# Weights and keys of the later stages prepared in steps inside the stage ahead

## The chip, the cores and the metric

The kernel runs on one core of a Trainium2 chip. The metric is the device time of one execution in microseconds (us), as the median of several runs. The engines are named PE (TensorE, the matrix unit; PEld is its weight load), DVE (VectorE), ACT (ScalarE), POOL (GpSimd) and SP (SyncE, which here only issues DMAs).

## The reference

The network has four layers, each an attention over a context of 1601 rows and a feed-forward part, all with 256 columns and residual sums over 2048 tokens. The parts that the change touches are these:

```python
def _L1_xattn_ref(h1, h2, mask, Wq, Wk, Wv):
    Q = jnp.einsum('bnd,hd->bnh', h1, Wq)
    K = jnp.einsum('bmd,hd->bmh', h2, Wk)
    V = jnp.einsum('bmd,od->bmo', h2, Wv)
    E = jnp.einsum('bnh,bmh->bnm', Q, K)
    E = jnp.where(mask == 0, jnp.float32(-10000000000.0), E)
    A = jax.nn.softmax(E / math.sqrt(HID), axis=2)
    return jnp.einsum('bnm,bmo->bno', A, V)

def _bitlinear(x, w_latent):                      # ffn of layer 1
    scale = jnp.clip(jnp.mean(jnp.abs(w_latent), axis=1, keepdims=True), 1e-05, None)
    tern = jnp.clip(jnp.round(w_latent / scale), -1.0, 1.0)
    return x @ (tern * scale).T
h = _bitlinear(x, w_fc) + gate * (x @ v.T @ fast_b.T @ u.T)
y = _bitlinear(jnp.maximum(h, 0.0) ** 2, w_proj)

def _ternary_linear(x, w):                        # ffn of layer 2
    alpha = jnp.mean(jnp.abs(w))
    w_t = jnp.sign(w) * (jnp.abs(w) > 0.5 * alpha)
    rms = jnp.sqrt(jnp.sum(x * x, axis=-1, keepdims=True)) / jnp.sqrt(d)
    return jnp.einsum('bsd,fd->bsf', x / (rms + EPS), w_t)
y = _ternary_linear(gelu(_ternary_linear(x, w_up)), w_down)
```

Layer 2's attention has the same form without a mask and with biases. Layer 3's attention has 16 heads of 16 columns, a mask, biases and an output projection; its masked keys get minus infinity. In both layers with a mask, every row of the drawn masks is zero for at least the first 1201 keys, so that only the last 400 of the 1601 context rows can count.

## The kernel before

The tokens lie in SBUF for the whole run, as 16 tiles of 128 rows (`x0` to `x15`), and the transposed context too (`ctxT`). Each stage goes over four chunks of 512 tokens. `norm` normalizes a chunk (statistics and scaling on DVE, the power on POOL), transposes it on PE into a PSUM buffer `pm` and lets ACT copy it out; with `split` it makes a high part on ACT and the rest on DVE. Each stage opens PSUM pools with `banks`: usually two buffers each of `psc` (scores or hidden units, two banks each), `pm` (small things) and `pa` (accumulators).

The stages follow each other in `network`. The first attention also looks at both masks, and a branch on the result (`tc.If`) picks the fast side: a tail attention over the last 400 keys (`attention1_tail`, L812 to L920), `ffn1` (L957), the attention over all keys (`attention1`, L654), `ffn2` (L1122), the last attention over the tail (`attention3_tail`, L1429), and `ffn3`. The other side is for other masks and doesn't run here.

In an attention, weights are transposed (`transpose_weight`, L211), keys and values made for all context rows, and then chunk by chunk: queries `q` with a bf16 copy `qb`, row maxima with bf16 matmuls (L881 or L748, reduced on DVE), scores (L903 or L780), the exponential on ACT, and value matmuls into `pa` (L913 or L800), whose result DVE divides and adds to `x`. The next chunk's queries and maxima come from a generator (`prepare`) that `step` advances a little between the current chunk's scores and value matmuls.

`ffn1` first loads its weights, then makes ternary weights on DVE (`ternary`: one comparison into `lo`, L928, and a comparison and subtraction, L929), transposes them on PE in bf16 (`transpose_up`, L938, and `transpose_down`, L950) with ACT copies out of PSUM, and prepares a low-rank term (`u`, `fast_b`, `b4`, `vh`, `vl`). Only then does the loop over chunks start, with low-rank matmuls (L1052), up matmuls (L1078) and down matmuls (L1115). `ffn2` does the same with thresholds over a whole matrix (L1141 to L1145), no low-rank term, a Gelu on ACT, and, per chunk, a sum of squares `sq` that POOL adds up (L1186) and PE sums over columns (L1197). `attention3_tail` transposes four weights (L211, L1503), makes keys with biases (L1511 to L1517) and values (L1521), and then walks over 16 units of a chunk and four heads each, projecting queries at L1545.

The order on each engine is made by a scheduler while the kernel is built, from the dependencies and the order in the source. Where a stage is opened with `manual_schedule(engines={PE})`, as the chunk loops of `ffn1` and `ffn2` are, PE keeps the source's order; in the last attention's loop all engines do. At run time each engine takes its instructions in the built order. Raw weights come through SP's DMA queue into `wraw`, a pool of three buffers used in turn (`weights`, L195), so a load waits until the weights three requests earlier have been used up. A pool opened inside a stage lies where the stage ahead had its own tiles, and its first uses wait until those are free:

```python
with ExitStack() as s:                                   # ffn1, L965
    self.banks(s)
    pool = s.enter_context(tc.tile_pool(name="f1", bufs=1))
...
net.attention1_tail("L1_xattn", masks[0])                # network, L1747
net.ffn1()
net.attention1("L2_xattn", bias=True)
net.ffn2()
net.attention3_tail(masks[1])
```

Of the kernel before, what the change touches and what calls it, by code (L numbers as in the profile page):

```python
# [15 lines left out]
P = 128  # L16
# [38 lines left out]
class Net:  # L55
# [44 lines left out]
    def psc(self):  # L100
        return self.ps_s.tile([P, 2, 512], F32, tag="s", name="psc")

# [102 lines left out]
    def transpose_weight(self, dst, raw, pad=None):  # L205

        nc = self.nc
        for kc in range(2):
# [5 lines left out]
            if pad:  # L214
                nc.scalar.copy(
                    dst[:, kc, :].rearrange("p (h e) -> p h e", e=32)[:, :, 0:16],
                    ps[:, :D].rearrange("p (h e) -> p h e", e=16),
                )
            else:
                nc.scalar.copy(dst[:, kc, :], ps[:, :D])  # L220

# [432 lines left out]
    def attention1(self, pre, mask=None, bias=False):  # L654
# [5 lines left out]
        with ExitStack() as s:  # L660
# [108 lines left out]
            for c in range(NCH):  # L769
# [25 lines left out]
                for i in range(TPC):  # L795
                    x = self.x[c * TPC + i]
                    acc = self.pa()
                    for kt in range(NKT):
# [5 lines left out]
                        if kt % 6 == 5:  # L804
                            step(nxt, 1)
                    ri = self.small.tile([P, 1], F32, name="ri1")
# [5 lines left out]
    def attention1_tail(self, pre, mask):  # L812
# [5 lines left out]
        with ExitStack() as s:  # L818
# [75 lines left out]
            for c in range(NCH):  # L894
# [14 lines left out]
                for i in range(TPC):  # L909
# [7 lines left out]
                    step(nxt, 1)  # L917
                    ri = self.small.tile([P, 1], F32, name="ri1")
# [12 lines left out]
    def transpose_up(self, dst, t):  # L931

        nc = self.nc
        for kc in range(2):
            for j in range(2):
# [5 lines left out]
                nc.scalar.copy(dst[:, kc, j * 512 : (j + 1) * 512], ps)  # L941

    def transpose_down(self, dst, t):

        nc = self.nc
        for f in range(0, 8, 2):
# [7 lines left out]
            nc.scalar.copy(dst[:, f : f + 2, :], ps.rearrange("p (k o) -> p k o", k=2))  # L954


    def ffn1(self):  # L957
# [6 lines left out]
        self.load_rows("L1_ffn_w_proj", F, wpr)  # L964
        with ExitStack() as s:  # L965
            self.banks(s)
            pool = s.enter_context(tc.tile_pool(name="f1", bufs=1))
            tp = s.enter_context(tc.tile_pool(name="f1t", bufs=3))
            hp = s.enter_context(tc.tile_pool(name="f1h", bufs=2))
            u = pool.tile([P, NF, R], F32, name="u")  # L970
            vv = pool.tile([R, D], F32, name="vv")
            fb = pool.tile([R, R], F32, name="fb")
            gate = pool.tile([R, 1], F32, name="gate")
            nc.sync.dma_start(u, a["L1_ffn_u"].rearrange("(o p) r -> p o r", p=P))
            nc.sync.dma_start(vv, a["L1_ffn_v"])
            nc.sync.dma_start(fb, a["L1_ffn_fast_b"])
            nc.sync.dma_start(gate, a["L1_ffn_gate"].partition_broadcast(R))

            def scales(view, n, cols):
                sc = pool.tile([P, n], F32, name=f"sc{n}")  # L980
                half = pool.tile([P, n], F32, name=f"half{n}")
                nhalf = pool.tile([P, n], F32, name=f"nhalf{n}")
                nc.vector.tensor_reduce(sc, view, AX.X, ALU.add, apply_absolute_value=True)
                nc.vector.tensor_scalar(sc, sc, 1.0 / cols, 1e-5, ALU.mult, ALU.max)
                nc.vector.tensor_scalar(half, sc, 0.5, None, ALU.mult)
                nc.vector.tensor_scalar(nhalf, sc, -0.5, None, ALU.mult)
                return sc, half, nhalf


            sc1, half, nhalf = scales(wfc, NF, D)  # L990
            rs1 = pool.tile([P, NF], F32, name="rs1")
            nc.vector.reciprocal(rs1, sc1)
            tfc = pool.tile([P, NF, D], BF16, name="tfc")
            for o in range(NF):
                self.ternary(tp, tfc[:, o, :], wfc[:, o, :], half[:, o : o + 1], nhalf[:, o : o + 1])
                nc.vector.tensor_scalar(u[:, o, :], u[:, o, :], rs1[:, o : o + 1], None, ALU.mult)
            wfT = pool.tile([P, 2, F], F32R, name="wfT")
            self.transpose_up(wfT, tfc)


            uT = pool.tile([R, F], F32, name="uT")
            b = pool.tile([R, F], F32, name="b")
            bh = pool.tile([R, 2, F], F32R, name="bh")
            b4 = pool.tile([P, F], F32R, name="b4")
            nc.gpsimd.memset(b4.bitcast(F32), 0.0)
            for j in range(2):
                ps = self.pm()
                for i in range(4):
                    nc.tensor.transpose(ps[0:R, i * P : (i + 1) * P], u[:, 4 * j + i, :], self.ident)
                nc.scalar.copy(uT[:, j * 512 : (j + 1) * 512], ps[0:R, :])  # L1010
                ps = self.pm()
                nc.tensor.matmul(ps[0:R, :], lhsT=fb, rhs=uT[:, j * 512 : (j + 1) * 512], start=True, stop=True)
                nc.vector.tensor_scalar(b[:, j * 512 : (j + 1) * 512], ps[0:R, :], gate, None, ALU.mult)
            nc.vector.tensor_copy(bh[:, 0, :], b)
            nc.vector.tensor_tensor(bh[:, 1, :], b, bh[:, 0, :].bitcast(F32), ALU.subtract)
            for k in range(4):
                nc.scalar.copy(b4[32 * k : 32 * k + R, :], bh[:, k % 2, :])

            v4 = pool.tile([P, 2, P], F32, name="v4")
            nc.gpsimd.memset(v4, 0.0)  # L1020
            vh = pool.tile([P, 2, P], F32R, name="vh")
# [100 lines left out]
    def ffn2(self):  # L1122
# [8 lines left out]
        with ExitStack() as s:  # L1131
# [23 lines left out]
            for o in range(2):  # L1155
                self.ternary(tp, tdn[:, o, :], wdn[:, o, :], half, nhalf)
# [638 lines left out]
```

## Time and profile before

| what | value |
| --- | --- |
| median of 3 runs | 2196.48 us (2189.63 to 2197.22) |
| the profiled execution | 2192.32 us, its span 2190.6 us |
| busy in the span | PE 1934.6 us (88%), DVE 1203.5 (55%), ACT 715.5 (33%), POOL 628.6 (29%) |
| chain that ended last | PE 65%, DVE 20%, ACT 5%, DMA 4% |
| mean granted PE clock | 0.946 |

The page shows one execution. Busy time is the time in which an engine executes; the rows of a stretch give it for each engine, with the number of instructions, and then PEclk, the granted clock of TensorE as a share of full speed. A line of the timeline has the start in us, the length in us, the engine, the source line and operation, what is written and read, and in brackets the idle time before it and what ended it. An f32 matmul shows as two records[...].

### The profile page before, as it was taken

Reading aid. Unit: us, or ns where it says so; the run is one execution under the profiler, and the core shown is the slowest. Engines: PE = TensorE matmul, PEld = TensorE weight load, DVE = VectorE, ACT = ScalarE, POOL = GpSimd, SP = SyncE. Lnnn points to the kernel's source line nnn. Section 1 sums busy time; section 2 is a strip of 40 time slices with the busy share of each in tenths; the row PEclk is TensorE's granted clock in tenths of the full one; section 3 lists DMA queues with packets and bytes.
Section 4 is the critical chain, followed back from the end, with each engine's and each line's share of the span. In section 5 each row is a group of like instructions: output and inputs, shape, how many; then the busy total and the mean of one; then the engine's idle time right before and its main releaser. Section 6 shows DMA issues by size and latency. Waiting matters only on the chain.

```text
span 2190.6 us, 22795 instructions
## 1 busy us (share of the span) xinstructions
PE 1934.6 (88%) x8831; PEld 963.6 (44%) x8841; DVE 1203.5 (55%) x2252; ACT 715.5 (33%) x968; POOL 628.6 (29%) x405
## 2 busy tenths in 40 slices
PE   7789999999998587789898789999977879889899
PEld 3233333333333433234444575455566622333487
DVE  4565656556462599985645553322156558677400
ACT  4554434444443100000011442111133246555422
POOL 1168878778686000000001011000013301111210
PEclk9799999999999599999998799999988889999999
DMA  8820000000000000000200000000000000000361
GB/s 280 274 82 1 1 1 1 1 1 1 1 1 0 0 1 1 1 0 0 68 0 14 27 1 22 1 0 1 0 1 1 5 1 1 1 1 1 107 199 62
DMA packets 39699, 63.51 MB, mean 29 GB/s; under 512 B 5134, under 2 KB 32159, under 8 KB 39583
## 3 DMA queue, kind: packets, MB, share of 16 engines
q1 hardware_dynamic: 37776, 60.33, 8.5%
q10 hardware_dynamic: 1806, 1.64, 0.2%
q8 instruction: 71, 1.16, 0.2%
q14 instruction: 46, 0.37, 0.1%
HBM read 59.87 MB, written 2.10 MB: 28 GB/s over the span
## 4 chain that ended last, share of the span: by engine, by line
PE 65%; DVE 20%; ACT 5%; DMA 4%; issue 4%; POOL 2%; SPq 0%; ACTq 0%; DVEq 0%; POOLq 0%
PE pa L468 7%; PE psc L456 5%; PE psc L641 5%; PE psc L780 4%; PE pa L800 4%; DVE ge L590 4%; PE psc L1578 3%; DVE mp L381 3%; DVE ge L592 3%; PE psc L1716 3%; PE pa L1727 3%; DVE ri L418 2%; ACT p L1585 2%; PE psc L454 2%; PE pm L1545 1%
## 5 line engine op out<-in xcount | busy, mean ns | idle before, releaser
L477 POOL TENSOR_TENSOR sp<-sp,p 128x1024 f32<-128x1024 f32 (+1 forms) x176 | 418.2, 2376 | 60.1 <-ACT p L461 49.5
L381 DVE TENSOR_REDUCE mp<-pm 128x1 f32<-128x512 f32 x384 | 242.6, 679 | 160.6 <-PE pm L376 159.8
L461 ACT ACTIVATE p<-psc 128x1024 f32<-128x1024 f32 (+1 forms) x208 | 212.7, 1022 | 259.5 <-PE psc L456 161.9
L456 PE MATMUL psc<-qT,kT 64*128 64x512 f32 (+1 forms) x832 | 221.7, 594 | 0.0
L468 PE MATMUL pa<-p,v 128*64 128x512 f32 (+1 forms) x832 | 202.4, 608 | 0.0
L607 PE MATMUL psc<-ge,pick 128*8 128x512 bf16 x512 | 142.3, 378 | 37.7 <-DVE ge L590 18.6
L1585 ACT ACTIVATE p<-psc 100x1024 f32<-100x1024 f32 x128 | 124.0, 1021 | 75.8 <-PE psc L1578 73.1
L1564 DVE TENSOR_REDUCE ms<-psc 128x2 bf16<-128x800 f32 x128 | 122.7, 981 | 43.3 <-PE psc L1560 41.4
L376 PE MATMUL pm<-kb,qb 64*128 64x512 bf16 x384 | 101.0, 391 | 27.2 <-DVE mp L381 25.7
L144 POOL TENSOR_SCALAR rstd<-mv 128x4 f32<-128x4 f32 x32 | 8.7, 272 | 358.1 <-DVE mv L140 358.1
L641 PE MATMUL psc<-w_e,xe 128*128 128x512 f32 x256 | 110.4, 593 | 0.0
L468 PEld LDWEIGHTS pa<-p,v 128*64 128x64 f32 (+1 forms) x832 | 50.9, 137 | 129.4 <-issue 126.4
L843 POOL MEMSET v<- 128x4 f32 x1 | 0.1, 104 | 364.3 <-DVE n_odd L294 364.3
L780 PE MATMUL psc<-q,kT 128*128 128x512 f32 (+1 forms) x208 | 102.2, 610 | 0.0
L590 DVE TENSOR_SCALAR ge<-bc,g 128x128 bf16<-128x128 f32 (+15 forms) x128 | 99.8, 780 | 1.8 <-ACT bc L584 1.8
L456 PEld LDWEIGHTS psc<-qT,kT 64*128 64x128 f32 (+1 forms) x832 | 86.0, 185 | 19.5 <-issue 6.3
L800 PE MATMUL pa<-v,p 128*128 128x257 f32 (+1 forms) x416 | 93.9, 381 | 0.2
L607 PEld LDWEIGHTS <-pick 128*8 128x8 bf16 x512 | 39.4, 85 | 117.1 <-issue 91.1
L454 PE MATMUL psc<-sh,negz 64*128 64x512 bf16 (+1 forms) x416 | 87.7, 384 | 3.6 <-ACT sh L403 3.5
L592 DVE TENSOR_SCALAR ge<-bc,g 128x1920 bf16<-128x1920 f32 (+14 forms) x120 | 89.4, 747 | 1.0 <-ACT bc L584 1.0
L753 DVE TENSOR_REDUCE mp<-pm 128x1 f32<-128x512 f32 x64 | 34.3, 570 | 99.9 <-PE pm L748 90.6
L648 DVE SCALAR_TENSOR_TENSOR x<-psc,g,x 128x256 f32<-128x256 f32 x128 | 61.9, 484 | 46.1 <-PE psc L641 42.5
(343 smaller groups left out, 3260.4 us busy)
## 6 DMA issues: line engine op xcount, KB each, us to landing
w<-in_L_ffn_w_dram SPq DMA_DIRECT2D x16, 1024.0 KB, 6.9
head<-in_mask_BxSxS_ik_dram SPq DMA_DIRECT2D x16, 600.5 KB, 4.0
head<-in_mask_1x1xSxS_ik_dram SPq DMA_DIRECT2D x16, 600.5 KB, 4.9
tail<-in_mask_BxSxS_ik_dram SPq DMA_DIRECT2D x16, 200.0 KB, 4.2
tail<-in_mask_1x1xSxS_ik_dram SPq DMA_DIRECT2D x16, 200.0 KB, 3.8
x<-in_x_dram SPq DMA_DIRECT2D x16, 128.0 KB, 3.7
w_e<-in_L_ffn_experts_dram SPq DMA_DIRECT2D x2, 1024.0 KB, 7.4
out_dram<-y SPq DMA_DIRECT2D x16, 128.0 KB, 2.5
```

The costliest lines, as they stand in the source:

```text
L381: nc.vector.tensor_reduce(mp[:, i, j, n : n + 1], pair[j][:, :wd], AX.X, ALU.max)
L456: nc.tensor.matmul(sc[:r, j, :], lhsT=kT[h, hp, kt * P : kt * P + r], rhs=q[h, :], start=False, stop=True,)
L461: nc.scalar.activation(p[:r], sc[:r], AF.Exp, scale=DH**-0.5)
L468: nc.tensor.matmul(acc[h, :], lhsT=v[:r, kt, hp * P + h.start : hp * P + h.stop], rhs=p[:r, j, :], start=kt == 0, stop=kt == NKT - 1,)
L477: nc.gpsimd.tensor_tensor(sums[:r], sums[:r], p[:r], ALU.add)
L590: nc.vector.tensor_scalar(ge[:, :hi], bc[:, :hi], own, None, ALU.is_lt)
L592: nc.vector.tensor_scalar(ge[:, hi:], bc[:, hi:], own, None, ALU.is_le)
L607: nc.tensor.matmul(rk[j // 2][0:E, j % 2, :], lhsT=pick[:, e, :], rhs=ge[:, j * CH : (j + 1) * CH], start=first, stop=last,)
L641: nc.tensor.matmul(sc[:, j, :], lhsT=xnT[t // TPC][:, kc, (t % TPC) * P : (t % TPC + 1) * P], rhs=ew[kc][:, half * 4 + 2 * j : half * 4 + ...
L780: nc.tensor.matmul(sc[:r, j, :], lhsT=kT[:, kc, ks], rhs=q[:, kc, :], start=kc == 0, stop=False)
L800: nc.tensor.matmul(acc[:, : D + 1], lhsT=p[:r, kt, i * P : (i + 1) * P], rhs=v[:r, kt, :], start=kt == 0, stop=kt == NKT - 1,)
L1585: nc.scalar.activation(p[:TR], sc[k][:TR], AF.Exp, scale=DH**-0.5)
```

## The change

The preparation of `ffn1`, of `ffn2` and of the last attention becomes a generator each: `ffn1_weights`, `ffn2_weights` and `attention3_keys`. Each loads its raw weights and opens its pools at its first step, in an `ExitStack` that `network` holds open around two stages; the later steps do the same work as before in small portions. The stage ahead gets the generator as `beside` and advances it: the tail attention by two steps after the value matmuls of each row block, the long attention by one, and `ffn2` by two for each pair of hidden blocks. `finish` runs what is left. The chunk loops themselves are the same. The raw weights are now requested before those of the attention in front of them. The last attention's values weight gets its own tile. The side of the branch that doesn't run here does its preparation at once, as before.

```diff
+    def finish(self, steps):
+        with ExitStack() as s:
+            self.banks(s)
+            drain(steps)
...
     def transpose_weight(self, dst, raw, pad=None):
+        drain(self.transpose_weight_steps(dst, raw, pad))
+    def transpose_weight_steps(self, dst, raw, pad=None):
...
+            yield
...
-    def attention1(self, pre, mask=None, bias=False):
+    def attention1(self, pre, mask=None, bias=False, beside=None):
...
+                    step(beside, 1)
                     ri = self.small.tile([P, 1], F32, name="ri1")
...
-    def attention1_tail(self, pre, mask):
+    def attention1_tail(self, pre, mask, beside=None):
...
                     step(nxt, 1)
+                    step(beside, 2)
...
-    def ffn1(self):
+    def ffn1_weights(self, s):
...
         self.load_rows("L1_ffn_w_fc", D, wfc)
         self.load_rows("L1_ffn_w_proj", F, wpr)
+        pool = s.enter_context(tc.tile_pool(name="f1", bufs=1))
+        tp = s.enter_context(tc.tile_pool(name="f1l", bufs=2))
...
+        yield
...
+        sc1, half, nhalf = scales(wfc, NF, D)
...
+        for o in range(NF):
+            self.ternary(tp, tfc[:, o, :], wfc[:, o, :], half[:, o : o + 1], nhalf[:, o : o + 1])
+            nc.vector.tensor_scalar(u[:, o, :], u[:, o, :], rs1[:, o : o + 1], None, ALU.mult)
+            if o % 2:
+                yield
+        wfT = pool.tile([P, 2, F], F32R, name="wfT")
+        yield from self.transpose_up(wfT, tfc)
...
+        for o in range(2):
+            self.ternary(tp, tpr[:, o, :], wpr[:, o, :], half[:, o : o + 1], nhalf[:, o : o + 1])
+            yield
+        wpT = pool.tile([P, NF, D], F32R, name="wpT")
+        yield from self.transpose_down(wpT, tpr)
...
+        self.f1 = wfT, wpT, b4, vh, vl, sc1, scb
+    def ffn1(self):
+        wfT, wpT, b4, vh, vl, sc1, scb = self.f1
...
+    def ffn2_weights(self, s):
...
+        for o in range(0, NF, 4):
+            yield
+            self.ternary(tp, tflat[:, o * D : (o + 4) * D], wflat[:, o * D : (o + 4) * D], half, nhalf)
...
+    def ffn2(self, beside=None):
...
                     if f == 2 and c + 1 < NCH:
                         nxt = self.norm(c + 1, rms=True, split=hp)
+                    step(beside, 2)
...
+    def attention3_keys(self, mask, s):
...
+        for w, n, pad in ((wkT, "Wk", True), (wqT, "Wq", True), (wvT, "Wv", None)):
+            yield from self.transpose_weight_steps(w, raw[n], pad)
...
+            nc.tensor.matmul(ps[:, :NTAIL], lhsT=to17, rhs=away, start=False, stop=True)
+            nc.scalar.activation(kT[:, g, :], ps[:, :NTAIL], AF.Identity, bias=kbias[:, g : g + 1])
+            nc.vector.tensor_copy(kb[:, g, :], kT[:, g, :])
+            yield
...
+        self.k3 = spread, qbias, bo, wqT, woT, kT, kb, v, ms
...
-        net.attention1_tail("L1_xattn", masks[0])
-        net.ffn1()
-        net.attention1("L2_xattn", bias=True)
-        net.ffn2()
-        net.attention3_tail(masks[1])
+        with ExitStack() as s1:
+            later = net.ffn1_weights(s1)
+            step(later, 1)
+            net.attention1_tail("L1_xattn", masks[0], later)
+            net.finish(later)
+            net.ffn1()
+        with ExitStack() as s2:
+            later = net.ffn2_weights(s2)
+            step(later, 1)
+            net.attention1("L2_xattn", bias=True, beside=later)
+            net.finish(later)
+            with ExitStack() as s3:
+                later = net.attention3_keys(masks[1], s3)
+                step(later, 1)
+                net.ffn2(later)
+                net.finish(later)
+                net.attention3_tail()
```

## The prediction

> **What bounds the kernel now.** I read the page first (PE busy 88% of the span, 65% of the chain that ended last; no DMA limit after the first tenth), then the chain of waits in order of time, which showed three stretches in which PE is not the chain: in front of the first ternary layer, in front of the second, and in front of the last attention. I cut the span there and asked for each stretch's busy times.
>
> ```profile
> core 0: us, PE busy (x) PEld busy (x) DVE busy (x) ACT busy (x) POOL busy (x), PEclk, DMA share, GB/s
> 1078.57:1094.40 15.83, 12.47 (x41) 7.55 (x41) 12.28 (x48) 3.19 (x9) 5.06 (x8) 0.68 0.69 232
> 1094.40:1189.61 95.21, 94.75 (x332) 48.60 (x332) 40.33 (x105) 16.95 (x24) 3.79 (x6) 1.00 0.00 1
> 1189.61:1217.39 27.78, 12.19 (x49) 4.71 (x49) 20.33 (x51) 9.74 (x15) 3.29 (x4) 0.53 0.26 79
> 1217.39:1330.40 113.01, 93.66 (x492) 78.75 (x493) 64.88 (x108) 47.46 (x71) 19.62 (x25) 0.89 0.01 1
> 1330.40:1608.39 277.99, 272.91 (x958) 154.47 (x968) 69.23 (x166) 43.28 (x61) 14.02 (x25) 0.99 0.02 4
> 1608.39:1625.38 16.99, 5.43 (x36) 3.95 (x37) 14.75 (x19) 3.96 (x8) 4.74 (x5) 0.58 0.00 0
> 1625.38:1738.00 112.62, 91.74 (x480) 79.99 (x481) 73.66 (x99) 44.04 (x66) 41.86 (x28) 0.82 0.02 3
> 1738.00:1759.50 21.50, 19.99 (x70) 11.24 (x70) 5.80 (x22) 6.95 (x14) 3.82 (x5) 0.85 0.02 1
> ```
>
> The rows are: start of the first tail attention, its body, weights of ffn1, ffn1, the long attention, weights of ffn2, ffn2, keys of the last attention. The first two weight stretches are DVE's (20.33 of 27.78 us, 14.75 of 16.99); the third is PE's own work (19.99 of 21.50). The hosts differ: both attentions have PE full at clock 1.00, so any PE instruction put there costs its whole length, while DVE is 42% and 25% busy. ffn2 has PE free for 20.9 us but a clock of 0.82.
>
> The timeline gives the edges of the stretches and what starts the first host:
>
> ```profile
> 1099.32 0.69 DVE L875 CAST qb<-pm 128x512 bf16<-128x512 f32 x1 [1.02 <-ACT q L874]
> 1189.61 2.29 DVE L983 TENSOR_REDUCE sc<-w_fc 128x8 f32<-128x2048 f32 x1
> 1203.11 1.28 DVE L929 SCALAR_TENSOR_TENSOR tpr<-w_pr,half,lo 128x1024 bf16<-128x1024 f32 x1
> 1220.14 0.80 PE L1052 MATMUL pm<-xnhi,vh 128*128 128x512 f32 x1 [0.79 <-DVE xnlo L180]
> 1628.14 0.79 PE L1174 MATMUL psc<-xnlo,wuT 128*128 128x512 f32 x1
> 1759.49 1.98 PE L1545 MATMUL pm<-xnT,w_l3q 128*128 128x512 f32 x4 [0.68 <-ACT xnT L177]
> ```
>
> In ffn2, PE by stretches of 4 us:
>
> ```profile
> 1649.00:1653.00 4.00, 1.27 (x8) 0.90 0.00 0
> 1653.00:1657.00 4.00, 4.00 (x14) 0.50 0.00 0
> ...
> 1673.00:1677.00 4.00, 1.65 (x11) 0.89 0.00 2
> 1677.00:1681.00 4.00, 2.30 (x12) 0.50 0.00 0
> 1681.00:1685.00 4.00, 4.00 (x17) 0.50 0.00 0
> ```
>
> At each chunk's end PE waits for GpSimd's sum of squares (3.76 us at 1648), then runs at half clock for 7 to 13 us.
>
> [...] 0.50 after 3.76 us idle, but also after two idles of 2.35 and 1.70 us close together. [...] here 406 GB/s were moved at 1085 to 1088 us. [...] The trace has the square at L1185 at 1.22 us alone and 3.29 us beside GpSimd. [...]
>
> **Part A, ffn1's weights into the first tail attention.** Removed: the last value matmul ends at 1189.49 and the first low-rank matmul starts at 1220.14, 30.65 us. What stays is transposing the normalized rows and splitting them: 8 transposes at full clock 1.03 us, one cast 0.59, one subtraction 0.65, about 2.4 with gaps. Gain 28.3. The first eight low-rank matmuls, 3.4 us at clock 0.50, would take 1.9: 1.5 more, 29.8.
>
> Added at the start. In the built order DVE has the reduction over w_fc, its eight ternary rows, the reduction over w_pr and both its ternary rows ahead of the casts of the first queries qb, and mixed among kb and v. I walked that list with the durations of before: rows normalized at 1085.1, statistics to 1086.0, reduction 2.25, scales and statistics 1.3, eight rows of 0.80 (lo, u, tfc) 6.4, statistics 1.0, kb 0.5, reduction 2.2, kb and v 0.9, scales and statistics 1.2, v 0.4, lo 0.7, v 0.4, tpr 1.2, v 0.4, then four rows of the next chunk behind their transposes 1.9, lo 0.7, statistics 0.5, tpr 1.2: the first qb starts at 1109.2 instead of 1097.60, the second at 1110.3 instead of 1099.32. PE's maxima (L881) stand behind qb, and the first shifts and exponentials behind them. So +11.3, and 0.7 for a colder PE: +12. The DMA order changes too: 2 MB of w_fc and w_pr and four small loads now go ahead of Wk, Wv and Wq, and Wq's issue waits for w_fc. An estimate from 2.1 MB at the 229 to 406 GB/s that the trace shows from 1079 to 1088 us: these three land near 1088, not 1082.3. That costs nothing only because kb waits for DVE until 1097. Without that cover it is 6 us.
>
> Added in the body, PE at full clock: 32 transposes in bf16 (four took 0.40 with their drain, 0.06 each) 1.9; 8 of u 1.0; two f32 matmuls with fast_b, 4 passes of 0.43, 1.7; the others 0.4: 5.0. PE's order is fixed, so waits for the two pm buffers, which ACT and DVE must empty (0.58 to 0.74 us each), come on top: between 0 and 5, I take 2. b4's four casts (4.2 us of ACT) stand ahead of the third chunk's exponentials, but fit before them. A = -29.8 + 12 + 7 = **-10.8**.
>
> **Part B, ffn2's weights into the long attention.** From the end of the last value matmul (1608.39) to the second up matmul (1628.14) are 19.75 us; transposes, cast and subtraction leave 2.45: gain 17.3. The first 16 up matmuls took 6.27 at half clock and 16 x 0.23 = 3.7 at full: 2.6 more. Added: 32 bf16 transposes 1.9, two threshold sums 0.5. DVE's 14 us of ternary work lies under value matmuls of 5.6 us per row block, DVE being 25% busy; waits 0.7. GpSimd's clearing of the next weights waits for tdn with a norm's rstd behind it, 2 us before that is due. B = -19.9 + 3.1 = **-16.8**.
>
> **Part C, keys into ffn2.** From the end of the sums over sq (1738.16) to the first query projection (1759.49) are 21.33 us. In the new program the transposes wait for all four updates of x (rms on GpSimd, reciprocal, 4 x 0.41: 3.5 us), then two rounds of transposes and ACT copies, about 2.8: 6.3 stay, gain 15.0. But those 20 us of PE work had warmed the array; the first two projections at half clock take 3.78 instead of 1.98 each: +3.6. The work comes back in ffn2: 12 + 8 f32 transposes 2.6, four key groups of 2.4, value matmuls 3.7: 15.9 us of PE, some 13 of it in the second chunk. That chunk has 5.7 us of PE idle, and work between the waits may keep the clock up (3 us). Against it, two key groups need pm buffers that DVE empties only after the split of xn, about 4 us. I take +9 (+2 if the gaps take it, +16 if nothing is hidden and the buffer waits are added). The bias load of ffn3 leaves the end of SP's queue: -0.6; ffn3's weights wait for the same GpSimd update as before. C = -15.0 + 3.6 + 9 - 0.6 = **-3.0**.
>
> **Sum**: -30.6. The profiled execution took 2192.32 us (span 2190.6 and 1.7 around it), so 2161.7. The three timed runs have their median 4.2 above it; a new median may lie anywhere in that spread, and I say 2163.
>
> **Rivals.** (1) The moved work costs what it saved in A and C: startup 18 instead of 12, because the cold array lasts through the first chunk, and ffn2 +16: -17.6, about 2176. For it: DVE is in order and the start has no other work for PE. Against: qb, not the clock, sets that start. (2) ffn2 absorbs the keys and stays warm: +2 instead of 9, and two restarts at half clock less, 3.5 each: -44.6, 2149. For it: 20.9 us idle and 0.82. Against: the inserted steps stand in the first two chunks, none just ahead of a wait for GpSimd. (3) Slower: the clock in the hosts. The first tail attention ran all its 95 us at 1.00; steps whose operands are late would cut PE's stream and hold it at 0.50. Each us at half clock loses 0.5; to lose the 30.6 and 11 more it takes about 84 us more at half clock, of 208 in the two short hosts. That gives 2205 or more. Against: each step's input is made at least one step ahead. (4) The steps don't spread: excluded for PE, whose built order has them between value and score matmuls; for DVE it is true in A, and priced.
>
> **How the numbers follow.** Main case 0.62 (its own range 2153 to 2173), (1) 0.18, (2) 0.14, (3) 0.04, nothing gained 0.02. The range 2147 to 2182 leaves out (3), the last, and halves of the tails of (1) and (2). About 0.5% (11 us) is what can be told from no change: faster means under 2185.5. Faster 0.93, same 0.03, slower 0.04.
>
> **What would show it.** A: no PE gap before the low-rank matmuls over 3 us; first qb near 1109; body 100 to 104 us at 1.00. B: up matmuls 2.5 us after the last value matmul, long attention 3 us longer. C: projections about 6 us after the sums over sq, ffn2 118 to 125 us. I am wrong if qb starts near 1098, if the body drops below clock 0.95, or if ffn2 keeps its 113 us.

## The result and the profile after

The changed kernel took 2162.94 us (median of 4 runs, 2161.41 to 2166.31) against 2194.51 us before, a ratio of 0.9868 with a 95% interval of 0.9851 to 0.9884. The prediction was 2163 us. Run again later beside other kernels it came to 0.9888 (0.9868 to 0.9908), so the medians put the gain at 26 to 32 us. The number was right, in part by luck: the stages below show that the forecast put 3.5 us too much on the change, and that a chance difference of 3.6 us in the time ahead of it made up for this.

First the windows of the changed kernel at the same edges as before (start of the tail attention, its body, ffn1, the long attention, ffn2, and the gap to the last attention's first projection; the two weight stretches have no row any more). Columns as in the table of before: length, then busy time of PE, PEld, DVE, ACT and POOL, PEclk, DMA share, GB/s.

```profile
1074.98:1090.81 15.83, 5.98 (x16) 3.51 (x17) 14.53 (x51) 2.15 (x6) 3.89 (x6) 0.51 0.69 211
1090.81:1201.17 110.36, 106.79 (x405) 55.16 (x404) 56.52 (x149) 28.19 (x41) 6.32 (x10) 0.99 0.07 23
1201.17:1314.40 113.23, 91.87 (x494) 77.55 (x492) 68.41 (x109) 47.09 (x70) 19.68 (x25) 0.89 0.01 1
1314.40:1594.41 280.01, 274.94 (x994) 156.50 (x1005) 78.50 (x185) 47.93 (x69) 17.95 (x29) 0.99 0.02 4
1594.41:1721.60 127.19, 101.41 (x541) 82.80 (x539) 75.39 (x119) 48.72 (x77) 45.18 (x32) 0.86 0.01 3
1721.60:1728.80 7.20, 2.24 (x9) 1.43 (x8) 2.00 (x6) 1.17 (x2) 1.21 (x2) 0.50 0.01 2
```

The tail attention is 126.19 us long instead of 111.04 (15.83 + 95.21), and in its first 15.83 us PE does 5.98 us of work where it did 12.47. ffn1 and the long attention have the length they had (113.23 for 113.01, 280.01 for 277.99). 27.78 and 16.99 us are gone. ffn2 grew from 112.62 to 127.19, and the keys' 21.50 shrank to 7.20.

The timeline of the changed kernel, with the instructions that answer to those shown of before (on DVE first, then the first low-rank matmul, the second up matmul, the last sums and the first query projection):

```profile
1083.09 2.25 DVE L999 TENSOR_REDUCE sc<-w_fc 128x8 f32<-128x2048 f32 x1
1094.12 2.25 DVE L999 TENSOR_REDUCE sc<-w_pr 128x2 f32<-128x2048 f32 x1
1103.67 1.27 DVE L943 SCALAR_TENSOR_TENSOR tpr<-w_pr,half,lo 128x1024 bf16<-128x1024 f32 x1
1104.86 0.68 DVE L888 CAST qb<-pm 128x512 bf16<-128x512 f32 x1
1111.95 0.68 DVE L243 CAST shift<-pm 1x512 bf16<-1x512 f32 x1 [0.89 <-PE pm L242]
1203.38 0.50 PE L1084 MATMUL pm<-xnhi,vh 128*128 128x512 f32 x1 [1.17 <-DVE xnlo L186]
1596.66 0.50 PE L1220 MATMUL psc<-xnlo,wuT 128*128 128x512 f32 x1 [0.35 <-DVE xnlo L186]
1718.06 3.57 PE L1244 MATMUL pm<-ones,sq 128*128 128x1 f32 x16 [3.82 <-POOL sq L1232]
1728.82 3.78 PE L1601 MATMUL pm<-xnT,w_l3q 128*128 128x512 f32 x4 [0.67 <-ACT xnT L183]
```

The last ternary row of w_pr (1103.67) stands right ahead of the first query cast, as the walk over DVE's list had it. The three gaps have shrunk to 2.4, 2.5 and 7.5 us (the last holds the update of x and the normalizing). The first projection runs at half clock (PEclk 0.50 from 1726 to 1730 us, 3.78 us for four records that took 1.98 before). Before, the clock had come up during the keys' matmuls: 0.50 in 1741 to 1744 us, 0.93 in 1744 to 1747, and 1.00 at the projection.

One thing outside of the change has to be taken off. Up to the branch both kernels are the same program, but single executions reach the tail attention's first DVE instruction (`keys`) at different times: 1078.3 us in the profile of before, 1074.7 in that of the changed kernel, 1082.6 when that was run again. So I compare stages from that instruction on. The span from there to the end is 1112.3 us before and 1085.2 (again: 1084.3) after: by the stages the change is worth 27 to 28 us, and 3.6 of the 30.7 us by which the first two profiled executions differ is chance.

### The profile page after: what moved, and what is told of

It reads as the page before. It is cut to its first block, busy times and chain, and to the rows that moved or that the text cites. A ratio compares the mean times of both kernels' runs of the same rounds, so it can differ in the third digit from the quotient of the medians.

```text
span 2159.9 us, 22786 instructions
## 1 busy us (share of the span) xinstructions
PE 1915.6 (89%) x8831; PEld 950.2 (44%) x8841; DVE 1197.5 (55%) x2252; ACT 714.8 (33%) x968; POOL 627.6 (29%) x405
## 3 DMA queue, kind: packets, MB, share of 16 engines
q8 instruction: 71, 1.16, 0.2%
## 5 line engine op out<-in xcount | busy, mean ns | idle before, releaser
L617 PE MATMUL psc<-ge,pick 128*8 128x512 bf16 x512 | 142.3, 378 | 37.7 <-DVE ge L600 19.3
L386 PE MATMUL pm<-kb,qb 64*128 64x512 bf16 x384 | 100.0, 390 | 26.7 <-DVE mp L391 25.1
L651 PE MATMUL psc<-w_e,xe 128*128 128x512 f32 x256 | 110.4, 593 | 0.0
L466 PEld LDWEIGHTS psc<-qT,kT 64*128 64x128 f32 (+1 forms) x832 | 85.5, 185 | 19.9 <-issue 6.6
```

Of the source, the lines that this page charges most:

```text
L386: nc.tensor.matmul(pair[j][:, :wd], lhsT=qb[h, i * P : (i + 1) * P], rhs=kb[h, hp, k0 : k0 + wd], start=True, stop=True,)
L466: nc.tensor.matmul(sc[:r, j, :], lhsT=kT[h, hp, kt * P : kt * P + r], rhs=q[h, :], start=False, stop=True,)
L617: nc.tensor.matmul(rk[j // 2][0:E, j % 2, :], lhsT=pick[:, e, :], rhs=ge[:, j * CH : (j + 1) * CH], start=first, stop=last,)
L651: nc.tensor.matmul(sc[:, j, :], lhsT=xnT[t // TPC][:, kc, (t % TPC) * P : (t % TPC + 1) * P], rhs=ew[kc][:, half * 4 + 2 * j : half * 4 + ...
```

## The experiments

This table has the stages of every run, from the first instruction of one stage to that of the next (us): the tail attention from `keys` to its last value matmul; from there to the first low-rank matmul; ffn1 to the first matmul of the next attention's keys; the long attention to its last value matmul; from there to the second up matmul; ffn2 to its last sum; from there to the first query projection; and the rest. The last columns are the sum of all these, and the ratio to before on the same chip with its interval.

| kernel | tail | gap 1 | ffn1 | long | gap 2 | ffn2 | gap 3 | rest | sum | ratio |
| --- | --- | --- | --- | --- | --- | --- | --- | --- | --- | --- |
| before | 110.8 | 31.0 | 110.3 | 277.6 | 20.1 | 109.7 | 21.7 | 431.1 | 1112.3 | 1 |
| changed | 126.3 | 2.4 | 111.0 | 279.8 | 2.5 | 124.6 | 7.5 | 431.1 | 1085.2 | 0.9868 (0.9851 to 0.9884) |
| changed, again | 126.3 | 2.4 | 110.1 | 279.9 | 2.5 | 124.6 | 7.6 | 430.9 | 1084.3 | 0.9888 (0.9868 to 0.9908) |
| A alone | 126.3 | 2.4 | 108.9 | 276.3 | 18.6 | 107.8 | 21.0 | 428.3 | 1089.6 | 0.9914 (0.9897 to 0.9930) |
| B alone | 112.2 | 23.7 | 111.7 | 280.1 | 2.4 | 108.5 | 21.2 | 428.8 | 1088.6 | 0.9914 (0.9897 to 0.9930) |
| C alone | 110.7 | 23.7 | 110.4 | 277.6 | 18.5 | 115.4 | 7.5 | 432.2 | 1096.0 | 0.9950 (0.9933 to 0.9967) |
| A and B | 126.2 | 2.4 | 108.7 | 280.1 | 2.4 | 108.5 | 21.1 | 430.3 | 1079.7 | 0.9877 (0.9860 to 0.9893) |
| regrouped only | 110.7 | 23.7 | 113.9 | 275.9 | 18.5 | 107.6 | 21.0 | 432.4 | 1103.7 | 0.9974 (0.9963 to 0.9985) |
| small operations late | 126.2 | 2.4 | 109.4 | 279.8 | 4.1 | 116.1 | 7.5 | 432.7 | 1078.2 | 0.9872 (0.9849 to 0.9894) |
| keys at chunk ends | 126.2 | 2.5 | 110.1 | 280.1 | 4.1 | 104.7 | 7.3 | 429.4 | 1064.4 | 0.9811 (0.9791 to 0.9831) |
| loads held | 116.3 | 2.4 | 110.1 | 280.0 | 2.5 | 122.3 | 7.5 | 432.4 | 1073.5 | 0.9839 (0.9819 to 0.9860) |
| held, and chunk ends | 116.0 | 2.4 | 110.1 | 279.9 | 4.1 | 104.7 | 7.4 | 432.3 | 1056.9 | 0.9769 (0.9748 to 0.9789) |
| and early norm | 116.1 | 2.5 | 110.0 | 279.9 | 4.1 | 104.9 | 3.8 | 432.4 | 1053.7 | 0.9740 (0.9719 to 0.9760) |

Most stages repeat to a few tenths; ffn1, the long attention and the rest vary by 2 to 5 us between kernels that have the same work there, and the part ahead of the branch by 8 us. There is one profile of before, and against it the sums show up to 7 us more gain than the medians do (A alone 22.7 against 18.4). So the sums serve to place a difference in a stage; what a kernel gains in all is taken from the ratios.

### Each part alone, and A with B

The edits are in `network` only: a part that is left out is run to its end by `finish` between the stages. A alone, for example:

```diff
+        net.attention1("L2_xattn", bias=True)
         with ExitStack() as s2:
-            later = net.ffn2_weights(s2)
-            step(later, 1)
-            net.attention1("L2_xattn", bias=True, beside=later)
-            net.finish(later)
-            with ExitStack() as s3:
-                later = net.attention3_keys(masks[1], s3)
-                step(later, 1)
-                net.ffn2(later)
-                net.finish(later)
-                net.attention3_tail()
+            net.finish(net.ffn2_weights(s2))
+            net.ffn2()
+        with ExitStack() as s3:
+            net.finish(net.attention3_keys(masks[1], s3))
+            net.attention3_tail()
```

> Only ffn1's weights go into the first tail attention; the weights of ffn2 and the last keys are prepared between the stages as before. My theory takes part A from the stages of the two traces: from the first DVE keys of the tail attention to its last value matmul +15.5 us, gap to the first low-rank matmul -28.6, ffn1 +0.7, so -12.4: about 2182 against 2194.5 before. The prediction had -10.8 for this part. The rival, that the 3.6 us by which the changed kernel was already ahead when the tail attention began belong to the change (a different layout of memory from the start), expects -16.

> Only ffn2's weights go into the long attention. Theory 1, that the 8.1 us stall of the second chunk's transposes in the first chunk of ffn2 comes from the keys' steps (part C), because they put two of the four squares behind two Gelus on ACT: here the four squares stand ahead of the first Gelu, the stall is at most 2.5 us, and B is +2.2 -17.6 -2.6 +2.2 = -15.8, about 2178.7. Theory 2, that a start of ffn2 straight after the attention makes the second chunk's normalization late with or without keys: the stall is again 6 to 9 us, B is -9 to -11, about 2184.5.

> Only the keys go into ffn2; ffn2's weights are made ahead of it as before, so the first up matmuls are cold and the squares of the second chunk stand ahead of the first Gelu. Both theories on the stall expect no stall above 3 us at the second chunk's transposes. Then C is -14.2 for the gap, 0 to +3.6 behind it and +7 to +9 in ffn2: -3 to -7, about 2189.5. If the keys' work costs in ffn2 what it saved even without the stall, this run is within 2 us of before.

> The changed kernel without part C. Theory 1 (the stall of 8.1 us comes with the keys' steps): A and B give -12.4 and -15.8, so -28 and about 2166, only 3 us or less above or below the changed kernel, and part C brings nothing. Theory 2 (the stall is B's): -22, about 2172, and part C brings 9 us.

Measured medians: A 2170.73, B 2170.14, C 2178.37, A and B 2162.04 us, against 2189.13 before: -18.4, -19.0, -10.8 and -27.1. All three parts alone gave more than expected, and together they would be 48 us, which the whole change does not give. The rival of the first expectation, a start that is faster because of the change, falls: `keys` came at 1078.4 us in A alone and at 1082.6 in the changed kernel run again, against 1078.3 before. A and B is as fast as the whole change within the noise: part C brings nothing that can be told on top of them. Two things follow from the table. Something is gained in every one of these kernels: gap 1 is 23.7 instead of 31.0 us in those that leave ffn1's weights where they were. And the keys cost ffn2 16.1 us when ffn2's weights have gone (124.6 against 108.5), but about 7.8 when they have not (115.4 against the 107.6 of the regrouped kernel below).

The stall behind the second is in the timeline of the changed kernel, at the start of ffn2. ACT has two of the four squares of the second chunk (L167) ahead of the first Gelu, and of the other two one behind two Gelus and a cast, the last behind both casts:

```profile
1598.39 0.42 ACT L167 ACTIVATE sq<-xn 128x256 bf16<-128x256 f32 x1
1598.92 1.28 ACT L1225 ACT_TABLE_LOAD   x1
1602.33 1.04 ACT L1225 ACTIVATE h<-psc 128x1024 f32<-128x1024 f32 x1
1603.25 0.43 ACT L167 ACTIVATE sq<-xn 128x256 bf16<-128x256 f32 x1
1603.65 1.05 ACT L1138 CAST rhi<-h 128x1024 fp32r<-128x1024 f32 x1
1604.58 0.43 ACT L167 ACTIVATE sq<-xn 128x256 bf16<-128x256 f32 x1
1605.18 1.64 POOL L195 TENSOR_TENSOR rms<-ss,phalf 128x4 f32<-128x4 f32 x1 [4.41 <-ACT sq L167]
1608.34 3.22 DVE L170 TENSOR_SCALAR xn<-xn,rmsi 128x256 f32<-128x256 f32 x4
1608.84 0.45 PE L179 MATMUL pm<-ident,xn 128*128 128x128 f32 x1 [8.11 <-DVE xn L170]
```

The rows were normalized by 1598.8, but GpSimd got its last square at 1605.1; PE, whose order is fixed in ffn2, stood for 8.11 us in front of the transposes. In the windows the stall and its bill, the half clock, follow each other:

```profile
1602.00:1606.00 4.00, 0.00 (x0) 0.00 (x0) 3.00 (x5) 3.11 (x7) 0.82 (x1) 0.81 0.00 0
1606.00:1610.00 4.00, 0.45 (x1) 0.18 (x1) 2.87 (x4) 0.00 (x0) 2.50 (x3) 0.50 0.00 0
1610.00:1614.00 4.00, 2.03 (x8) 1.50 (x9) 3.22 (x8) 1.74 (x5) 0.89 (x1) 0.50 0.00 0
1614.00:1618.00 4.00, 3.83 (x11) 2.86 (x11) 0.92 (x2) 1.75 (x8) 0.00 (x0) 0.50 0.03 6
```

With A and B and no keys, the four squares are together, ahead of the table load and the Gelus, and the same transposes wait for 1.43 us:

```profile
1600.21 0.42 ACT L167 ACTIVATE sq<-xn 128x256 bf16<-128x256 f32 x1
1600.74 1.28 ACT L1225 ACT_TABLE_LOAD   x1
1603.98 1.46 PE L179 MATMUL pm<-ident,xn 128*128 128x128 f32 x8 [1.43 <-DVE xn L170]
```

So theory 1 stands: the stall needs the keys' steps. It needs part B too, since C alone has the four squares ahead and lost only 7.8 us in ffn2.

### What every kernel has in common: the regrouping

All three preparations are generators in pools opened ahead of the stage, and all are run to their end between the stages. Nothing is moved into a stage.

```diff
+        net.attention1_tail("L1_xattn", masks[0])
         with ExitStack() as s1:
-            later = net.ffn1_weights(s1)
-            step(later, 1)
-            net.attention1_tail("L1_xattn", masks[0], later)
-            net.finish(later)
+            net.finish(net.ffn1_weights(s1))
             net.ffn1()
...
```

> Nothing is moved into the stage ahead: each of the three preparations is a generator that is run to its end between the stages, in pools opened ahead of the stage and with PSUM buffers of its own. The runs of the parts alone add up to 48 us where the whole change gave 29, so about 10 us must be in every one of them. Theory: that share is the regrouping, because the first chunk of ffn1 is then transposed right after the last value matmul and not behind the weights (gap to the low-rank matmuls 23.7 instead of 31.0 us in the runs of part B and part C alone), with 1.5 and 2 us more in front of and in ffn2: -11 us, ratio about 0.995. Rival: the parts disturb each other, and without steps the time is that of before.

Measured 2184.26 us against 2189.53 (10 runs against 13): 5.3 us faster, half of what was expected and clearly not nothing (the stage sums have 8.6). PE of this kernel in front of ffn1:

```profile
1191.18 1.04 PE L179 MATMUL pm<-ident,xn 128*128 128x128 f32 x8
1214.14 0.59 PE L965 MATMUL pm<-identb,tpr 128*128 128x128 bf16 x4 [0.32 <-DVE v L1047]
1214.67 0.79 PE L1084 MATMUL pm<-xnhi,vh 128*128 128x512 f32 x1
1220.08 0.79 PE L1110 MATMUL psc<-xnhi,wfT 128*128 128x512 f32 x1 [0.52 <-ACT scb L1067]
```

The first chunk is transposed right behind the last value matmul, in time that PE waits anyway; before, that stood behind the weights, at 1217.39. The low-rank matmuls come 7.3 us earlier, but 1.8 of these go again, because the last transposes of weights now stand behind them and the first up matmul waits 0.52 us for `scb`: it starts 29.1 us after the last value matmul instead of 34.6. What follows in ffn1 is longer in this profile, but not in those of B and C, which have the same work there. Counting the 5.3 us once, A adds 13.1, B 13.7 and C 5.5 to it. A and B would then give 32.1 us together; they gave 27.1. Each of these medians is uncertain by 2.4 to 3.6 us, so this may be noise. Whether the separate PSUM buffers or the place of the pools made the other order possible was not separated.

### The keys' small operations later

Eight small DVE operations of the keys' first step (row sums, `spread`, `away`, `to17`, the bias sums) run at the start of ffn2 in the changed kernel. Moved behind the transposed weights, they leave the four squares together, ahead of the first Gelu.

```diff
 def attention3_keys(self, mask, s):
-        nc.vector.tensor_reduce(row16, self.ident[:, DH::32], AX.X, ALU.add)
-        nc.vector.tensor_copy(spread, self.ident[:, DH::32].unsqueeze(2).to_broadcast([P, G, 32]))
...
-        nc.vector.tensor_tensor(qbias, qbias, row17.to_broadcast([P, G]), ALU.add)
...
             nc.scalar.copy(woT[:, g : g + 2, :], ps.rearrange("p (k o) -> p k o", k=2))
             yield
+        nc.vector.tensor_reduce(row16, self.ident[:, DH::32], AX.X, ALU.add)
+        nc.vector.tensor_copy(spread, self.ident[:, DH::32].unsqueeze(2).to_broadcast([P, G, 32]))
...
+        nc.vector.tensor_tensor(qbias, qbias, row17.to_broadcast([P, G]), ALU.add)
         for g in range(G):
```

> The changed kernel with the keys' small DVE operations (row sums, spread, away, bias sums) moved from the first step behind the transposed weights. In the built order the four squares of the second chunk then stand ahead of the first Gelu on ACT again. Theory: the stall of 8.1 us in the first chunk shrinks to 2 or 3 us and with it some work at half clock, ffn2 takes 117 to 119 us instead of 124.6, ratio about 0.984. Rival: the stall is only a place where PE pays for the keys' work, and the time comes back at the first chunk's end; ratio 0.986 to 0.988 as for the whole change.

The first run gave 2162.93 us, 0.9880 (0.9860 to 0.9900): no better than the changed kernel's first ratio, although ffn2 took 116.2 us instead of 124.6; the theory had expected 0.984. Since these two were compared across chips, both were run again side by side.

> The keys' small DVE operations behind the transposed weights, once more beside the changed kernel: its stages behind the branch were 7.8 us shorter than those of the changed kernel, but its ratio (0.988) was not lower. Theory: on one chip it is 5 to 8 us faster than the changed kernel. Rival: the stages ahead of the branch are slower with it, and the two take the same time within 2 us.

> The changed kernel itself once more, on the same chip as the next three. The stages behind the branch took 27.1 us less than before in its profiled execution, and the stages ahead of the branch, the same program, ended 3.6 us earlier there by chance. Theory: ratio 0.987 to 0.988. If the start belonged to the change, the ratio is again 0.986 or less.

Now 2158.87 against 2164.91 us: 6.0 us between the medians, and 6.1 between the sums of stages. The ratios' intervals overlap, and lie in the first rival's range too, so the stages carry this verdict: ffn2 -8.5, gap 2 +1.6, in both runs. The rival "it comes back" falls by them. The earlier 0.9868 owed more to the kernel before (2194.51 us there, 2189 to 2191 in all later measurements) than to the changed one (2162.94 and 2164.91).

### The keys at the ends of the chunks

```diff
-                    step(beside, 2)
                 for f, parts in late:
                     self.down(acc, f, parts, wdT, NF)
+                step(beside, (8, 2, 2, 4)[c])
                 ps = self.pm()
...
-                step(later, 1)
+                step(later, 2)
                 net.ffn2(later)
```

The small operations are late in this one too.

> As the run before, and the keys' steps stand at each chunk's end of ffn2, ahead of the sums that wait for GpSimd (8, 2, 2 and 4 steps, about 2.6, 5.0, 5.0 and 3.7 us of PE), instead of two steps after each pair of hidden blocks. Theory: they fill four idle times of 3.8 us and keep the clock up, so ffn2 takes 106 to 111 us, as without the keys, and the ratio is about 0.980. Rival: with only two small PSUM buffers the steps wait for ACT and DVE, the idle time is not shorter than the steps, and ffn2 is at 117 us or more.

Measured 2148.36 us, 0.9811. ffn2 with all of the keys in it takes 104.7 us, less than the 109.7 it took without them before (107.6 to 108.5 in the regrouped kernels without keys), and a little less than the theory's 106 to 111. The small-operations kernel of the same measurement took 2162.93 us, so the new places are worth 14.6 us. PE at the ends of the first two chunks:

```profile
1624.84 0.60 PE L220 MATMUL pm<-ident,w_l 128*128 128x128 f32 x4
1627.48 1.09 PE L1531 MATMUL pm<-ident,w_l3k 128*128 128x128 f32 x8 [0.19 <-ACT wvT L229]
1628.90 1.92 PE L1244 MATMUL pm<-ones,sq 128*128 128x1 f32 x16 [0.33 <-POOL sq L1232]
1653.40 1.50 PE L1555 MATMUL pm<-ctxT,w_l3k 128*128 128x400 f32 x4
1657.24 0.93 PE L1559 MATMUL pm<-away,to 1*128 1x400 f32 x2
1658.11 2.05 PE L1244 MATMUL pm<-ones,sq 128*128 128x1 f32 x16
```

and the clock there:

```profile
1624.00:1628.00 4.00, 3.38 (x26) 2.52 (x26) 2.29 (x1) 1.94 (x6) 2.77 (x2) 1.00 0.00 2
1656.00:1660.00 4.00, 4.00 (x22) 2.56 (x21) 0.37 (x1) 1.00 (x2) 0.31 (x1) 0.98 0.02 4
1660.00:1664.00 4.00, 4.00 (x12) 3.20 (x13) 1.42 (x6) 0.32 (x1) 2.38 (x4) 0.60 0.00 0
```

The 3.8 us in which PE waited for GpSimd are full, the clock stays up through the sums (1.00 in 1628 to 1632, 0.98 in 1656 to 1660), and their sixteen records (two for each of eight f32 matmuls) take 1.92 to 2.05 us where they took 3.15 to 3.57 before. The clock does not stay up everywhere: behind the sums of the second chunk it is at half for about 3.4 us (an estimate from the 0.98 and the 0.60). The same comes behind the third chunk's sums (0.89 in 1684 to 1688, 0.68 in 1688 to 1692), and in the first chunk some 9 us behind them, after PE has waited 1.20 and 2.21 us for xn (0.92 in 1636 to 1640, 0.66 in 1640 to 1644, with up matmuls of 0.63 us that took 0.39 ahead of it); before, each chunk had 7 to 14 us at half clock, estimated in the same way. Ahead of the sums, with an idle time of 0.33 us in the first chunk and none in the second in place of 3.8, the clock holds. Behind the second chunk's sums it fell without any idle time just ahead: PE was busy for all of the 12 us from 1652 to 1664. What brought it down there no run shows.

### The loads of ffn1 held

```diff
 def ffn1_weights(self, s):
...
+        yield
+        if self.held is not None:
+            for w in (wfc, wpr):
+                nc.scalar.copy(w[:, 0, 0:1], self.held[:, 0, 0:1])
         self.load_rows("L1_ffn_w_fc", D, wfc)
...
 def attention1_tail(self, pre, mask, beside=None):
             drain(prepare(0, made))
+            self.held = made[0][0]
+            step(beside, 1)
```

> The changed kernel with the loads of both weights of ffn1 held until the first chunk's queries are written (a one-column write from q into each weight's place, which the load then overwrites). On DVE all of the ternary work then stands behind the first shift. Theory: the first queries come at the time of before, about 10 us earlier, and the tail attention takes 117 us to its last value matmul instead of 126.3; ratio about 0.983. Rival: the ternary work has no room in the body, queries and maxima of the second chunk wait for it, and the time is that of the whole change within 3 us.

Measured 2153.54 us, 0.9839; the tail attention takes 116.3 us instead of 126.3. DVE of this kernel (`keys` at 1074.4):

```profile
1093.72 0.69 DVE L889 CAST qb<-pm 128x512 bf16<-128x512 f32 x1 [1.41 <-ACT q L888]
1101.69 0.68 DVE L244 CAST shift<-pm 1x512 bf16<-1x512 f32 x1 [0.90 <-PE pm L243]
1102.29 2.26 DVE L1006 TENSOR_REDUCE sc<-w_fc 128x8 f32<-128x2048 f32 x1
```

The first query cast comes 19.3 us after `keys`, as before; the shift 27.3 us after it (27.3 before, 37.2 in the changed kernel). All of the ternary work is behind it, and the body had room for it: 5.5 us over before remain, PE's own share of the added work (in the tail attention PE is busy for 112.80 us, before 107.22). So the 10 us at the start come from loading and making ffn1's weights early. The hold undoes two things at once, DVE's order and the order of the loads, and no run parts them. That DVE set the time is read from the changed kernel, where it has no idle time over 0.31 us from 1081 on and the last ternary row of w_pr ends at 1104.9, as the first query cast begins. The loads come close behind it: the first keys (`kT`, the copy ahead of `kb`) were ready 17.0 us after `keys` there and 10.0 before, so by an estimate from these figures moving DVE's work alone would have left some 7 of the 10 us.

### Both together, and a version beyond

> The loads held until the first queries are written, the small operations late and the keys' steps at the chunks' ends, together. Theory: the two gains lie in different stages and add up: 9.9 us in the tail attention and 19.9 us in ffn2 off the changed kernel, ratio about 0.975, 2134 us against 2189.5. If they disturb each other, 0.978 or more.

Measured 2138.94 us, 0.9769: the sum of stages falls by 27.4 us against the changed kernel run beside it, the medians by 26.0, where 29.8 were expected. In their stages the gains add up: the tail attention is 10.3 us shorter and ffn2 19.9.

The last one also normalizes the last attention's first chunk inside ffn2:

```diff
                     if f == 2 and c + 1 < NCH:
                         nxt = self.norm(c + 1, rms=True, split=hp)
+                    if f == 4 and c + 1 == NCH and beside is not None:
+                        self.xnT0 = self.norm(0)
...
-            drain(self.norm_steps(0, xn))
-            xnT[0] = xn.pop()
+            xnT[0] = self.xnT0
```

> As the run before, and the first chunk of the last attention is normalized and transposed within ffn2's last chunk, since its rows are final after ffn2's first. Theory: of the 7.3 us between the sums and the first query projection some 6.5 go, 1.3 us of transposes come back in ffn2, and the two projections run at full clock (1.98 instead of 3.75 us each): 7 to 9 us less than the run before, ratio 0.971 to 0.972. Rival: the normalization is late in ffn2's last chunk and PE waits there for what it saved: no difference over 2 us.

Measured 2132.45 us, 0.9740 (0.9719 to 0.9760), the fastest of all: 58 us under before on that chip. The medians differ by 6.5 us from the run before, the sums of stages by 3.2, and the two intervals overlap, so the size is uncertain; 7 to 9 us and a ratio of 0.971 to 0.972 were expected. Gap 3 went to 3.8 us, not below 1:

```profile
1697.64 1.95 PE L1253 MATMUL pm<-ones,sq 128*128 128x1 f32 x16 [0.19 <-POOL sq L1239]
1703.12 3.68 PE L1610 MATMUL pm<-xnT,w_l3q 128*128 128x512 f32 x4 [3.54 <-DVE x L1262]
1708.29 1.98 PE L1610 MATMUL pm<-xnT,w_l3q 128*128 128x512 f32 x4 [1.48 <-ACT q L1615]
```

The projection, whose input is ready, still waits for the last update of x. The update reads ffn2's accumulators, and the last attention's PSUM buffers are opened where these lie; that the buffer is what it waits for is argued from the releaser, not tried. The first projection is still at half clock (3.68 us), the second back at 1.98. The sums ahead of the wait of 3.54 us took 1.95 us, as at full clock, so the clock fell behind them; these lines don't show when. In the kernel with the keys at the chunks' ends the last record of these sums began at 1710.2, and the clock was 0.88 in 1708 to 1712 and 0.50 in 1712 to 1716. By an estimate from these figures it fell there at 1711.0, some 0.5 us behind the sums, when the wait had hardly begun.

## Why the prediction was right, and where not

**The sum.** -30.6 us were forecast on the profiled execution; the stages gave -27.1 (and -28.0 in the second profile). The two profiled executions differ by 30.7 us, as forecast, because 3.6 us ahead of the branch came on top by chance. The forecast of 2163 thus hit a figure that chance had helped, inside its own range either way; the second measurement, 26.0 us by the medians, is 4.6 us short of it.

**A, -10.8: measured -12.4** (tail +15.5, gap 1 -28.6, ffn1 +0.7). Gap 28.3 was 28.6. Startup +12 was +10.0 at the shift and +10.9 at the first query cast; the walk over DVE's list is confirmed, and with the loads held the 10 us are gone. The body, +7, was +5.5. The DMA order was hidden as said: Wk's transposes began 9.9 us after `keys` instead of 2.6, PE having stood idle for 10.82 us until Wk's load ended (3.62 before), and the first key cast followed the last ternary row of w_fc (1092.8) by less than 1 us; the cover was needed, since the first `kT` came 7.0 us later (6 were estimated). The 1.5 us from warm low-rank matmuls did not reach the end: the eight took 2.0 instead of 3.6 us, but PE then waited 1.16 us for y, and ffn1 was no shorter.

**What the prediction did not ask** is how much of the gain needs no moving at all: 5.3 us, most of it in gap 1. It priced each gap as one piece, from the end of one stage to the start of the next, which is right for the whole change, and so never asked what the regrouping alone would do.

**B, -16.8: measured -15.4 in the stages** (long attention +2.2 for +3.1, gap 2 -17.6 for -17.3). The 2.6 us of clock for the first up matmuls did not show as a shorter ffn2: 108.5 us in the runs with B and no keys, 107.6 in the regrouped one. By the medians B is worth 13.7 on top of the regrouping and 8.7 on top of A.

**C, -3.0: between no gain and a loss of some 5 us.** Gap 3, -15.0, was -14.2 and the two cold projections were 3.78 and 3.73 us, as the +3.6 had it; neither this nor the -0.6 for the bias load can be seen in the rest (431.1 us before and after), which varies by 4. The step that failed is ffn2: +9 was forecast, and it measured +14.9 against before and +16.1 against A and B, the value that rival 1 had for it, though not by rival 1's way. The prediction looked for the cost in the second chunk, at pm buffers. Of the +14.9 over before, 9.8 fell into the first chunk (sums over at 36.5 us after the second up matmul, 26.7 before) and 6.1 into the second, while the other two gave 1 us back. In the second the forecast was near: PE was busy for 33.23 of 35.07 us (before 23.24 of 28.98), so its idle time took 3.9 us of the keys' work, and its wait for the split of xn was 1.59 us, not 4. C alone, without the stall, cost ffn2 7.8 us. The first chunk's part comes from ACT: the steps' eight small DVE operations changed the order in which four squares and two Gelus were put, and PE waited for it. The prediction walked DVE's list for A and never walked ACT's for C.

**The rivals.** (1) came true for ffn2 alone; the startup was 10 to 11 us, not 18. (2), that ffn2 takes the keys for nothing and stays warm, was false for the change, and true, but for some 3.4 us at half clock in each of three chunks (the estimate above), as soon as the steps stood ahead of the sums: "none just ahead of a wait for GpSimd" was the right reason. (3), half clock in the hosts, did not come: the body ran at 0.99 and the long attention at 0.99. (4) held for DVE at the start of A, as it was priced. The signs that were named held: qb near 1109 (1104.86, which is 1108.5 on the clock of before), no gap over 3 us ahead of the low-rank matmuls, projections 6 us after the sums (7.2). Only ffn2 was outside, 127 us for 118 to 125.

## What to carry to other kernels

When work is moved beside another stage, walk the built order of every engine that it touches, not only of the one it loads most: eight small operations on DVE turned the order on ACT here, and PE stood for 8.11 us. Put the moved steps just ahead of a wait that the critical engine already has: in ffn2 they cost no time there (104.7 us with the keys' steps, 107.6 to 108.5 without), and the clock held through the sums that follow (1.00 and 0.98). Hold their inputs back if an engine's order would otherwise put them ahead of what starts the stage: here the hold, which also put the loads later, was worth 10 us. And try the regrouping without the move: part of a gain can be in the order that it sets free.

## What the runs showed of the hardware

Identical instructions ahead of the branch ended 8 us apart in single executions (`keys` at 1074.4 to 1082.6 us), as much as several edits here move; counting from a common instruction brought the tail attention of seven runs with the same work into 0.1 us. In the changed kernel the sixteen records of a chunk's column sums, each with one output column, took 1.95 us at clock 1.00 (second chunk, from 1666.30) and 3.57 at 0.50 (last chunk, from 1718.06), nearly the factor of the clock; PEld, the weight load, was busy for 1.86 and 3.49 us of these. The granted clock fell to half behind such sums without an idle time of PE: PE waited 0.24 us ahead of those at 1666.30 and was busy from there to 1672.5, at 1.00 to 1668.25, 0.82 to 1670 and 0.50 to 1672.5, with up matmuls of 0.63 us where 0.39 follow. In the kernel with the keys at the chunks' ends it was 0.98 in 1656 to 1660 us and 0.60 in 1660 to 1664, PE busy throughout. So a PE that is always busy was no sign here that the clock stays up.
